# Selections moved behind the squares, and a smaller last step, in a patch-matching convolution kernel

## The chip, the cores and the metric

The kernel runs on one core of one Trainium2 chip. A core has five engines that run side by side, each through its own instructions in order: TensorE (PE in the profile; its weight loads are PEld), VectorE (DVE), ScalarE (ACT), GpSimd (POOL) and SyncE (SP). The last two mostly issue transfers here, which 16 DMA engines carry out. TensorE writes its products to a small memory of eight banks, PSUM, from which ScalarE or VectorE must copy them before a bank is used again.

The metric is the time of one execution in microseconds on the device. The kernel before took 7137.65 us (median of 11 runs, 7121.78 to 7152.27).

## The reference

Eight images of 32 channels and 128 x 128 pixels pass through two layers. What matters here is the first:

```
xb = _patch_match_stack(x)                    # x normalised; 8 shifted copies: 256 channels
dct = _conv(xb, dct_w, groups=C)
h = relu(_conv(_conv(xb, w1), w2, groups=CK, pad=1))
h = relu(_conv(_conv(h, w3), w4, groups=CK, pad=1))
wiener = sigmoid(_conv(_conv(h, w5), w6, groups=CK, pad=1))
filt = _conv(wiener * dct, inv_dct_w, groups=C)
x = x + _conv(filt, agg_w)
```

The patch match looks, for each pixel, at 25 offsets (dy, dx from -2 to 2), sums the squared difference to the shifted image over the channels and over a 3x3 patch, takes the 8 offsets of least cost, and gathers the 8 shifted copies. w1, w3 and w5 are pointwise (1x1, 256 to 256 channels), w2, w4 and w6 are 3x3 filters of one channel each. The second layer normalises the result by groups of channels, filters every channel with one 5x5 kernel and adds that.

## The kernel before

**Tiling.** The rows of an image are worked off eight at a time (R = 8); 16 such steps (NS = 16) and a seventeenth, n = NS, make an image. The seventeenth is there because a 3x3 filter needs the row below: stage i (1, 2, 3: one pointwise and one 3x3 filter each) lags the input by i rows in all, so that the last step has only i rows of stage i left to put out. The steps of all images form one list; step s of the outer loop runs stage 1 on step s, stage 2 on step s - 1, stage 3 on step s - 2, and the end (stage "0") on step s - 2. So around a change of image the stages work on different images, and there is one step of the outer loop in which stage 1 does its n = NS, one for stage 2 and one for stage 3.

**Substeps.** A step of the outer loop has four substeps, i = 3, 2, 1, 0. The order of what TensorE, VectorE and ScalarE do is the order in which the program emits it (`manual_schedule`); GpSimd and SyncE get theirs from a scheduler. A substep i of 3, 2, 1 emits:

- `pointwise_v` (TensorE pv, L637; ScalarE copies tv, L645): the pointwise product for channels 128 to 255, and the first tap of their 3x3 filter (ScalarE, L685);
- waiting small tasks of TensorE (queue "P"), and the cost matmuls pd of the squares made before (queue "Q");
- **the selection** (`gather_select`, ScalarE L584 and L585) for unit u + 1, and the loads of unit u + 3 (`gather_load`, GpSimd L570 for ib, L555 for xt);
- `tick`: a share of the patch match of the next image on VectorE (queue "D"), among it the differences df (L410), in pairs; n = 0 to 2 of an image hold the most of them;
- the other eight taps on VectorE (L688), 128 channels of eight rows each;
- `pointwise_t` (TensorE p, L660; ScalarE copies t, L667; SyncE transfers t<-t, L670 and L672): the pointwise product for channels 0 to 127, laid out by rows in four groups of 32 partitions;
- `gather_pixels` for unit u (TensorE pg, L599; ScalarE copy xb, L606): 88 small products of the shifted pixels with the selection;
- the 3x3 filter of channels 0 to 127 of the substep before, on TensorE (pw, L709), into two banks that exist once (`ps_dw`, one buffer for each of two tags);
- the squares of df (queue "A", ScalarE L418); the relu or sigmoid of the substep before for channels 128 to 255 (ScalarE L692);
- **the evictions** of pw through relu or sigmoid (ScalarE L721), which free those two banks.

Substep 3 has no pw (the substep before it, 0, has no 3x3 part). In substep 0, TensorE multiplies with the dct (pc, L757; the product with acc on VectorE, L760), then does pw of stage 1, and pg behind it; the final products pa (L773) come in the next substep.

**Units.** A gather unit is four rows and four of the eight copies. Units are numbered through; u counts one on in every substep. Step n = NS has none, so that for one step per image nothing is gathered. A selection turns the index tile ib (loaded from DRAM for all 128 partitions; five buffers) into a 0/1 tile sel (four buffers): `ib = (ib - partition)^2`, then `sel = relu(1 - ib)`, for two tiles of 128 x 1024 each. The selection for unit u + 1 is made one substep ahead of its pg.

The emission around the change, before:

```
run("Q")
if s < len(steps):
    unit(gather_select, u + 1)
    unit(gather_load, u + 3)
    tick(b, i)
```

**The last step before.** At n = NS `pointwise_t` works on one row of each of four row groups (nb = 1), of which i - 1 count; the rest of t is set to zero by GpSimd (L669). `depthwise_v` filters four rows, of which i count. `depthwise_t` computes, for u = 0 and 1, two rows each (`[:, :, :nb]`), four in all.

Of the kernel before, what the change touches and what calls it, by code (L numbers as in the profile page):

```python
# [17 lines left out]
C, K, H, W = 32, 8, 128, 128  # L18
CK = C * K
NO = 25  # L20
R = 8
NS = H // R
# [21 lines left out]
def bm3d_conv_preact(  # L44
# [16 lines left out]
    nc = tc.nc  # L61
# [85 lines left out]
    with tc.tile_pool(name="setup", bufs=1) as sp, tc.tile_pool(  # L147
# [3 lines left out]
        for n, w in enumerate((w2, w4, w6)):  # L151
# [6 lines left out]
            for u in range(2):  # L158
                for dy in range(3):
                    s = slice(C * (u + dy), C * (u + dy + 1))  # L160
# [10 lines left out]
        for name, w in (("w1", w1), ("w3", w3), ("w5", w5)):  # L171
            t = sp.tile([P, 2, CK], F32, name=f"nat_{name}", tag=f"nat_{name}")
            nc.sync.dma_start(t, w.rearrange("(m p) i a b -> p m (i a b)", p=P))
            if name == "w1":

                nat, t = t, sp.tile([P, 2, CK], F32, name="w1_kc")
# [6 lines left out]
        for name, dst in (("w1", lw1), ("w3", lw3), ("w5", lw5)):  # L183
            for g in range(2):
                ps = spp.tile([P, CK], F32, name=f"ps_{name}_{g}", tag="ps")
# [461 lines left out]
    def pointwise_t(i, b, n, lhsT, src):  # L647
        t = tb[i - 1]
        nb = 2 if n < NS else 1
        if n == NS and i == 1:  # L650
            nc.gpsimd.memset(t[:, :, 2], 0.0)
        else:
            for q in range(2):
                ps = ps_x.tile([P, 2, 2, W], F32, name=f"p{i}_{b}_{n}_{q}", tag="x")
                for e in range(2):
                    s = slice(C * (2 * q + e), C * (2 * q + e + 1))
                    for g in range(2):
                        rows = src(g)
                        for r in range(4):
                            nc.tensor.matmul(  # L660
                                ps[C * r : C * (r + 1), e, :nb],
                                lhsT[:, g, s],
                                rows[:, r : r + 4 * nb - 3 : 4],
                                start=g == 0,
                                stop=g == 1,
                            )
                nc.scalar.copy(t[:, 2 * q : 2 * q + 2, 2 : 2 + nb], ps[:, :, :nb])  # L667
            for r in range(i - 1) if n == 0 else range(i - 1, 4) if n == NS else ():
                nc.gpsimd.memset(t[C * r : C * (r + 1), :, 2], 0.0)  # L669
        nc.sync.dma_start(t[64:P, :, 0:nb], t[0:64, :, 2 : 2 + nb])  # L670
        if nb == 2:
            nc.sync.dma_start(t[0:64, :, 1], t[64:P, :, 2])  # L672

    def depthwise_v(i, b, n):
        v = tv[i - 1]
        nr = R if n < NS else 4
        out_ = accp.tile([P, R, W], F32, name=f"acc{i}_{b}_{n}_1", tag=f"acc{i}1")
        acc = out_[:, :nr]
        for k, (dy, dx) in enumerate(
            ((1, 1), (0, 0), (0, 1), (0, 2), (1, 0), (1, 2), (2, 0), (2, 1), (2, 2))  # L680
        ):
            tap = dwv[:, i - 1, 3 * dy + dx : 3 * dy + dx + 1]
            rows = v[:, dy : dy + nr, dx : dx + W]
            if k == 0:
                nc.scalar.activation(acc, rows, AF.Copy, scale=tap)  # L685
                yield out_
            else:
                nc.vector.scalar_tensor_tensor(  # L688
                    acc, rows, tap, acc, op0=ALU.mult, op1=ALU.add
                )  # L690
        yield
        nc.scalar.activation(acc, acc, funcs[i - 1])  # L692
        yield
        rows_before_v(i, b, n)

    def depthwise_t(i, b, n):
        t = tb[i - 1].rearrange("p q (h k) w -> p q h k w", k=2)
        nb = 2 if n < NS else 1

        pt = [  # L700
            ps_dw.tile([P, 2, 2, W], F32, name=f"pw{i}_{b}_{n}_{u}", tag=f"dw{u}")
            for u in range(2)
        ]
        for u in range(2):
            hi = 96 if u == 0 else P
            for dx in (0, -1, 1):
                xa, xz = max(0, -dx), min(W, W - dx)
                for j in range(4):
                    nc.tensor.matmul(  # L709
                        pt[u][C * j : C * (j + 1), :, :nb, xa:xz],  # L710
                        dwd[0:hi, i - 1, u, j, dx + 1],
                        t[0:hi, j, :, :nb, xa + dx : xz + dx],
                        start=dx == 0,
                        stop=True,
                        skip_group_check=True,
                    )
        yield 1
        acc = accp.tile([P, R, W], F32, name=f"acc{i}_{b}_{n}_0", tag=f"acc{i}0")
        rows = acc.rearrange("p (k e) w -> p e k w", e=4)
        for u in range(2):  # L720
            nc.scalar.activation(rows[:, u:4:2, :nb], pt[u][:, :, :nb], funcs[i - 1])  # L721
        rows_before_t(i, b, n)
        accs[i, b, n][0] = acc

# [131 lines left out]
    steps = [(b, n) for b in range(NB) for n in range(NS + 1)]  # L856
# [7 lines left out]
    lws, funcs = (lw1, lw3, lw5), (AF.Relu, AF.Relu, AF.Sigmoid)  # L864
    accs, fins = {}, {}

    def unit(stage, u):
        if 0 <= u < len(units) and units[u]:
            if stage is gather_load:
                at = (units[u][0], units[u][1] % 8 // 2)  # L870
                until(lambda: at in ready, 4.0)
            stage(*units[u])
# [28 lines left out]
    with tc.manual_schedule(engines=ORDERED):  # L901
        push(prep(0))
        push(mixes())
        xbd[0] = dram.tile([P, 2, H, W], F32, name="xbd_0", tag="xbd")
        for i in range(3):
            nc.gpsimd.memset(tb[i][0:64, :, 0], 0.0)
        for u in range(7):
            unit(gather_load, u)
            unit(gather_select, u - 2)
            unit(gather_pixels, u - 3)  # L910
        u = 4

        dt = dv = kept = iter(())

        later = lambda: None

        for s in range(len(steps) + 2):
            if s < len(steps):
                b, n = steps[s]
                if s == 2:  # L920
                    push(bands())
                if n == (0 if b else 4) and b + 1 < NB:
                    until(lambda: b in ready, 4.0)
                    push(prep(b + 1))
                if n == NS - 1 and b + 1 < NB:
                    until(lambda: b + 1 in ready, 4.0)
                    xbd[b + 1] = dram.tile([P, 2, H, W], F32, name=f"xbd_{b+1}", tag="xbd")
            for i in (3, 2, 1, 0):
                si = s - (i - 1 if i else 2)
                live = 0 <= si < len(steps)  # L930
                new_v = new_t = iter(())
                if live:
                    bi, ni = steps[si]

                if live and i:
                    src = source(i, bi, ni)
                    pointwise_v(i, bi, ni, lws[i - 1], src)
                    new_v, new_t = depthwise_v(i, bi, ni), depthwise_t(i, bi, ni)
                    accs[i, bi, ni] = [None, next(new_v)]
                later()  # L940
                later = lambda: None
                if live and not i:
                    if ni == 0:
                        x1d[bi] = dram.tile([C, H, W], F32, name=f"x1d_{bi}", tag="x1d")
                        stats[bi] = work.tile([P, NS + 1, 6], F32, name=f"stat_{bi}", tag="stat")
                    xr, xf, j0, j1 = fins.pop(si)
                run("P")
                if live and not i:
                    final_dct(bi, ni, accs[3, bi, ni], xf, j0, j1)

                run("Q")
                if s < len(steps):
                    unit(gather_select, u + 1)
                    unit(gather_load, u + 3)
                    tick(b, i)
                next(new_v, None)
                if live and i:
                    pointwise_t(i, bi, ni, lws[i - 1], src)
                next(kept, None)
                if not i:  # L960
                    next(dt, None)
                if s < len(steps):
                    unit(gather_pixels, u)
                    u += 1
                if i:
                    next(dt, None)
                run("A")
                next(dv, None)
                next(dt, None)
                kept, dv, dt = dv, new_v, new_t  # L970
                if live and not i:
                    later = partial(end, bi, ni, xr, j0, j1)
                if not i and 0 <= s - 1 < len(steps):
                    fins[s - 1] = final_load(*steps[s - 1])
        next(kept, None)
        later()
        until(lambda: NB - 1 in done, 4.0)
# [62 lines left out]
```

## Time and profile before

| what | us |
|---|---|
| median of 11 runs | 7137.65 (7121.78 to 7152.27) |
| the profiled execution | 7160.98 |
| its span | 7159.2 |
| TensorE busy in the span | 6716.4 |
| VectorE busy | 5840.3 |
| ScalarE busy | 5064.3 |
| selections, L584 and L585, 1024 each | 1165.5 and 1084.3 |
| copies t, L667, 128 x 512 | 413.3 (768, mean 580 ns) |
| evictions L721, 128 x 512 | 437.8 (768, mean 597 ns) |

The profiler follows one execution. A row of a group gives the line of the program, the engine, the operation, output and input, the shape and the count, then busy time and the mean of one, then the idle time of the engine ahead of it and what ended it. In a wait row the engine and line named first waited for the one behind the arrow; behind the colon stand the total, the number and the longest. In the order of time each row starts with its start and its length; a bracket at its end gives the idle time of that engine ahead of it. "issue" is idle time for which the profile shows no cause. The clock that is granted to TensorE is given as a share of full speed.

Steps take some 55 us where the next image is being matched and 46 us in the last image; around a change of image they take 39 to 53 us.

### The profile page before, as it was taken

To read this page: it belongs to the slowest core of one execution; us is meant where nothing else is said; L and a number is where in the kernel's file an instruction comes from. 1 tells how busy PE (TensorE), PEld (TensorE's weight loads), DVE (VectorE), ACT (ScalarE), POOL (GpSimd) and SP (SyncE) were. 2 spreads that over 40 slices of the span, in tenths; PEclk is the share of its full clock that TensorE was granted. 3 is DMA by queue.
4 is the path that set the end of the run, shared out by engine and by line. 5 is a ranking of instruction groups with operands and counts; after the bars stand their busy time and mean duration, and the time that the engine had idled before them with its cause. 6 is when DMAs were issued, how large, how long until landed. Compare 5 with 4: busy or idle time off the path is not lost. (4 is left out here: it accounts for less than half of the span.)

```text
span 7159.2 us, 229485 instructions
## 1 busy us (share of the span) xinstructions
PE 6716.4 (94%) x100226; PEld 3165.6 (44%) x100226; DVE 5840.3 (82%) x8606; ACT 5064.3 (71%) x6706; POOL 2744.4 (38%) x4599
## 2 busy tenths in 40 slices
PE   4699899999999999999999999999999999999997
PEld 1344444444444444444444444444444444444443
DVE  6689878888888888888888898888988789767775
ACT  4587668677686777867677776877768677676762
POOL 6244336333353343533335333443336333332222
PEclk8799999999999999999999999999999999999999
DMA  3566656666566575656656666565656656555652
GB/s 80 129 145 147 148 131 148 147 146 149 135 150 148 140 161 130 160 142 147 152 124 162 144 149 138 139 158 148 153 133 150 147 142 150 130 142 141 147 136 65
DMA packets 765484, 1007.70 MB, mean 141 GB/s; under 512 B 215008, under 2 KB 578592, under 8 KB 764480
## 3 DMA queue, kind: packets, MB, share of 16 engines
q0 software_dynamic: 378400, 733.67, 41.8%
q1 hardware_dynamic: 381056, 256.86, 16.9%
q8 instruction: 788, 12.91, 0.8%
q10 hardware_dynamic: 5024, 2.49, 0.2%
q14 instruction: 216, 1.77, 0.1%
HBM read 542.24 MB, written 217.01 MB: 106 GB/s over the span
## 5 line engine op out<-in xcount | busy, mean ns | idle before, releaser
L688 DVE SCALAR_TENSOR_TENSOR acc<-tv,dwv,acc 128x1024 f32<-128x1024 f32 (+1 forms) x3264 | 4083.5, 1252 | 224.5 <-ACT acc L685 110.9
L709 PE MATMUL pw<-t,dwd 128*32 128x508 f32 (+6 forms) x19584 | 2191.5, 594 | 167.1 <-DMA t<-t 115.4
L709 PEld LDWEIGHTS pw<-t,dwd 128*32 128x32 f32 (+1 forms) x19584 | 700.8, 112 | 1418.0 <-issue 1237.9
L570 POOL DMA_DIRECT2D ib<-idxd x1024 | 578.9, 566 | 1894.0 <-ACT sel L585 1774.0
L584 ACT ACTIVATE ib<-ib,nplace 128x1024 bf16<-128x1024 bf16 x1024 | 1165.5, 1138 | 25.2 <-DMA ib<-idxd 25.2
L585 ACT ACTIVATE sel<-ib 128x1024 f32<-128x1024 bf16 x1024 | 1084.3, 1059 | 32.6
L660 PE MATMUL p<-acc,lw 128*32 128x256 f32 x17408 | 992.5, 374 | 10.8 <-issue 10.4
L637 PE MATMUL pv<-acc,lw 128*128 128x512 f32 (+1 forms) x2112 | 977.7, 605 | 8.8 <-DVE acc L760 4.8
L606 ACT COPY xb<-pg 128x512 f32<-128x512 f32 x512 | 304.0, 594 | 724.9 <-PE pg L599 724.0
L645 ACT COPY tv<-pv 128x512 f32<-128x512 f32 (+2 forms) x784 | 445.1, 584 | 493.7 <-PE pv L637 473.2
L660 PEld LDWEIGHTS p<-acc,lw 128*32 128x32 f32 x17408 | 560.8, 110 | 430.4 <-issue 82.1
L721 ACT ACTIVATE acc<-pw 128x512 f32<-128x512 f32 (+1 forms) x816 | 453.4, 584 | 354.1 <-PE pw L709 353.9
L599 PEld LDWEIGHTS pg<-sel,xt 128*32 128x32 f32 x45056 | 591.3, 111 | 233.0 <-issue 133.9
L599 PE MATMUL pg<-sel,xt 128*32 128x48 f32 x45056 | 594.6, 206 | 90.5 <-issue 60.8
L780 DVE TENSOR_TENSOR xr<-xr,pa 128x256 f32<-128x256 f32 (+2 forms) x136 | 55.0, 405 | 732.3 <-PE pa L773 732.3
L637 PEld LDWEIGHTS pv<-acc,lw 128*128 128x128 f32 x2112 | 383.3, 192 | 410.6 <-issue 379.7
L410 DVE TENSOR_TENSOR df<-xn 128x786 f32<-128x786 f32 (+2 forms) x576 | 528.5, 967 | 19.0 <-PE pd L425 18.0
L667 ACT COPY t<-p 128x512 f32<-128x512 f32 x800 | 423.6, 571 | 115.9 <-PE p L660 112.5
L418 ACT ACTIVATE df<-df 128x786 f32<-128x786 f32 (+2 forms) x576 | 460.8, 861 | 47.0 <-DVE df L410 45.8
L685 ACT ACTIVATE acc<-tv,dwv 128x1024 f32<-128x1024 f32 (+1 forms) x408 | 459.7, 1127 | 45.8 <-PE pa L773 31.6
L637 PE MATMUL pv<-xb,lw 128*128 128x512 f32 x1024 | 475.8, 607 | 0.0
L757 PE MATMUL pc<-xf,ldct 128*128 128x512 f32 (+2 forms) x1056 | 470.9, 588 | 0.0
(128 smaller groups left out, 6397.6 us busy)
## 6 DMA issues: line engine op xcount, KB each, us to landing
ib<-idxd POOLq DMA_DIRECT2D x1024, 256.0 KB, 4.3
xbd<-xb POOLq DMA_DIRECT2D x128, 1024.0 KB, 7.9
xf<-xbd POOLq DMA_DIRECT2D x480, 256.0 KB, 9.3
t<-t SPq DMA_DIRECT2D x792, 128.0 KB, 4.9
t<-t SPq DMA_DIRECT2D x384, 256.0 KB, 4.9
tv<-tv SPq DMA_DIRECT2D x384, 130.0 KB, 4.1
xt<-xtd POOLq DMA_DIRECT2D x240, 176.0 KB, 5.2
xl<-xs POOLq DMA_DIRECT2D x256, 64.0 KB, 2.7
```

Source lines behind the costliest of these rows:

```text
L410: nc.vector.tensor_sub(df[:, :, ca:cz], xn[:, r0 : r0 + SR, ca:cz], xn[:, r0 + dy : r0 + dy + SR, ca + dx : cz + dx],)
L418: nc.scalar.activation(df[:, :, ca:cz], df[:, :, ca:cz], AF.Square)
L570: nc.gpsimd.dma_start(ib.rearrange("p k y x -> p (k y x)"), idxd[b][s4 // 8, s4 % 8, 4 * k0 : 4 * k0 + 8] .rearrange("k x -> (k x)") .part ...
L584: nc.scalar.activation(ib, ib, AF.Square, bias=nplace)
L585: nc.scalar.activation(sel, ib, AF.Relu, scale=-1.0, bias=1.0)
L599: nc.tensor.matmul(pg[C * j : C * (j + 1), :, xa:xz], xt[:, t], sels[j // 2][:, j % 2, :, xa:xz], start=True, stop=True,)
L637: nc.tensor.matmul(ps[:, :hr], lhsT[:, g, P:CK], src(g)[:, h : h + hr], start=g == 0, stop=g == 1,)
L660: nc.tensor.matmul(ps[C * r : C * (r + 1), e, :nb], lhsT[:, g, s], rows[:, r : r + 4 * nb - 3 : 4], start=g == 0, stop=g == 1,)
L685: nc.scalar.activation(acc, rows, AF.Copy, scale=tap)
L688: nc.vector.scalar_tensor_tensor(acc, rows, tap, acc, op0=ALU.mult, op1=ALU.add)
L709: nc.tensor.matmul(pt[u][C * j : C * (j + 1), :, :nb, xa:xz], dwd[0:hi, i - 1, u, j, dx + 1], t[0:hi, j, :, :nb, xa + dx : xz + dx], start ...
L757: nc.tensor.matmul(ps[:, : z - a], ldct[:, m], xf[:, m, a:z], start=True, stop=True)
```

## The change

The selection of unit u + 1 is emitted later in its substep: behind pg, the squares (`run("A")`) and the activation L692 (`next(dv, None)`), and in front of the evictions L721 (the last `next(dt, None)`). The loads of unit u + 3 stay where they were. At n = NS, `pointwise_t` computes and copies only the i - 1 row groups that count, `depthwise_v` filters i rows in place of four, and `depthwise_t` computes for u = 0 and 1 as many rows as lie among those i: (1, 0) for stage 1, (1, 1) for stage 2, (2, 1) for stage 3.

```
     def pointwise_t(i, b, n, lhsT, src):
         t = tb[i - 1]
         nb = 2 if n < NS else 1
+        nr = 4 if n < NS else i - 1
...
-                        for r in range(4):
+                        for r in range(nr):
                             nc.tensor.matmul(
                                 ps[C * r : C * (r + 1), e, :nb],
...
-                nc.scalar.copy(t[:, 2 * q : 2 * q + 2, 2 : 2 + nb], ps[:, :, :nb])
+                nc.scalar.copy(
+                    t[: C * nr, 2 * q : 2 * q + 2, 2 : 2 + nb], ps[: C * nr, :, :nb]
+                )
...
     def depthwise_v(i, b, n):
         v = tv[i - 1]
-        nr = R if n < NS else 4
+        nr = R if n < NS else i
...
+        nh = [2 if n < NS else (i + 1 - u) // 2 for u in range(2)]
         for u in range(2):
             hi = 96 if u == 0 else P
             for dx in (0, -1, 1):
                 xa, xz = max(0, -dx), min(W, W - dx)
-                for j in range(4):
+                for j in range(4 if nh[u] else 0):
                     nc.tensor.matmul(
-                        pt[u][C * j : C * (j + 1), :, :nb, xa:xz],
+                        pt[u][C * j : C * (j + 1), : nh[u], :nb, xa:xz],
                         dwd[0:hi, i - 1, u, j, dx + 1],
-                        t[0:hi, j, :, :nb, xa + dx : xz + dx],
+                        t[0:hi, j, : nh[u], :nb, xa + dx : xz + dx],
...
         for u in range(2):
-            nc.scalar.activation(rows[:, u:4:2, :nb], pt[u][:, :, :nb], funcs[i - 1])
+            if nh[u]:
+                nc.scalar.activation(
+                    rows[:, u : u + 2 * nh[u] - 1 : 2, :nb], pt[u][:, : nh[u], :nb], funcs[i - 1]
+                )
...
                 run("Q")
                 if s < len(steps):
-                    unit(gather_select, u + 1)
                     unit(gather_load, u + 3)
                     tick(b, i)
...
                 if s < len(steps):
                     unit(gather_pixels, u)
-                    u += 1
                 if i:
                     next(dt, None)
                 run("A")
                 next(dv, None)
+                if s < len(steps):
+                    unit(gather_select, u + 1)
+                    u += 1
                 next(dt, None)
```

More of the change, by code (lines that the diff above doesn't have):

```diff
@@ L649, in pointwise_t @@
         nb = 2 if n < NS else 1
+        nr = 4 if n < NS else i - 1
         if n == NS and i == 1:
@@ L658, in pointwise_t @@
                         rows = src(g)
-                        for r in range(4):
+                        for r in range(nr):
                             nc.tensor.matmul(
@@ L666, in pointwise_t @@
                             )
-                nc.scalar.copy(t[:, 2 * q : 2 * q + 2, 2 : 2 + nb], ps[:, :, :nb])
+                nc.scalar.copy(
+                    t[: C * nr, 2 * q : 2 * q + 2, 2 : 2 + nb], ps[: C * nr, :, :nb]
+                )
             for r in range(i - 1) if n == 0 else range(i - 1, 4) if n == NS else ():
@@ L675, in depthwise_v @@
         v = tv[i - 1]
-        nr = R if n < NS else 4
+        nr = R if n < NS else i
         out_ = accp.tile([P, R, W], F32, name=f"acc{i}_{b}_{n}_1", tag=f"acc{i}1")
@@ L703, in depthwise_t @@
         ]
+        nh = [2 if n < NS else (i + 1 - u) // 2 for u in range(2)]
         for u in range(2):
@@ L707, in depthwise_t @@
                 xa, xz = max(0, -dx), min(W, W - dx)
-                for j in range(4):
+                for j in range(4 if nh[u] else 0):
                     nc.tensor.matmul(
-                        pt[u][C * j : C * (j + 1), :, :nb, xa:xz],
+                        pt[u][C * j : C * (j + 1), : nh[u], :nb, xa:xz],
                         dwd[0:hi, i - 1, u, j, dx + 1],
-                        t[0:hi, j, :, :nb, xa + dx : xz + dx],
+                        t[0:hi, j, : nh[u], :nb, xa + dx : xz + dx],
                         start=dx == 0,
@@ L720, in depthwise_t @@
         for u in range(2):
-            nc.scalar.activation(rows[:, u:4:2, :nb], pt[u][:, :, :nb], funcs[i - 1])
+            if nh[u]:
+                nc.scalar.activation(
+                    rows[:, u : u + 2 * nh[u] - 1 : 2, :nb], pt[u][:, : nh[u], :nb], funcs[i - 1]
+                )
         rows_before_t(i, b, n)
@@ L952, in bm3d_conv_preact @@
                 if s < len(steps):
-                    unit(gather_select, u + 1)
                     unit(gather_load, u + 3)
@@ L963, in bm3d_conv_preact @@
                     unit(gather_pixels, u)
-                    u += 1
                 if i:
@@ L968, in bm3d_conv_preact @@
                 next(dv, None)
+                if s < len(steps):
+                    unit(gather_select, u + 1)
+                    u += 1
                 next(dt, None)
```

## The prediction

> **What bounds the kernel now.** I read the shares of busy time first, then the stretches of the span, then who waited for whom on TensorE, and last single substeps in order of time.
>
> ```profile
> span 7159.2 us, 229485 instructions
> PE 6716.4 (94%) x100226; PEld 3165.6 (44%) x100226; DVE 5840.3 (82%) x8606; ACT 5064.3 (71%) x6706; POOL 2744.4 (38%) x4599
> ```
>
> TensorE is busy 94% of the span. The next view cuts the span at the image changes (length, then busy time of PE, PEld, DVE, ACT, POOL, then the clock granted to TensorE).
>
> ```profile
> 1900.00:2050.00 150.00, 136.45 (x2328) 71.09 (x2319) 123.49 (x133) 122.41 (x171) 71.66 (x118) 0.97 0.54 138
> 2050.00:2760.00 710.00, 691.87 (x10150) 321.26 (x10142) 602.55 (x939) 507.08 (x666) 270.03 (x454) 1.00 0.63 148
> ```
>
> In the body of an image TensorE is 97% busy (691.87 of 710); around an image change 91% (136.45 of 150), and ScalarE 82%. The work of TensorE sets the end, and what can be won is its idle time: some 18 us in each body and 13.5 at each of seven changes. What it waits for between 300 and 7010 us (total, times, longest):
>
> ```profile
> PE pw L709 <- DMA t<-t: 95.9, 43, 7.5
> PE pg L599 <- issue: 60.8, 41, 4.2
> PE pw L709 <- issue: 27.3, 16, 5.4
> PE pw L709 <- DMA tv<-tv: 10.0, 4, 4.2
> ```
>
> The first row is what the change can reach; "issue" waits on nothing that is shown, and I leave it. One such wait, from substep 1 into substep 0 (start, length):
>
> ```profile
> 3089.67 3.63 PE L660 MATMUL p<-xb,lw 128*32 128x256 f32 x64
> 3093.62 1.06 ACT L585 ACTIVATE sel<-ib 128x1024 f32<-128x1024 bf16 x1
> 3094.58 1.05 ACT L667 COPY t<-p 128x512 f32<-128x512 f32 x2
> 3096.30 0.61 SPq L672 DMA_DIRECT2D t<-t  x1
> 3105.85 5.33 PE L709 MATMUL pw<-t,dwd 96*32 96x512 f32 x48 [2.67 <-DMA t<-t]
> ```
>
> The matmuls p end at 3093.30, but the copies t of ScalarE stand behind the selections and end at 3095.63, 2.3 us later; the transfers follow, and the 3x3 matmuls start 2.67 us late.
>
> A wait costs more than its length. In the windows after a wait of 2.84 us (ending at 5695.16) the clock column reads 0.50:
>
> ```profile
> 5690.00:5695.00 5.00, 2.32 (x6) 0.76 (x4) 4.49 (x7) 3.53 (x4) 1.79 (x3) 1.00 1.13 143
> 5695.00:5700.00 5.00, 4.84 (x24) 1.35 (x28) 2.97 (x17) 0.00 (x0) 1.60 (x3) 0.50 0.23 62
> ```
>
> Those 48 matmuls took 8.60 us, where 5.33 is usual. Over all groups of 48 that follow a wait above 0.3 us between 300 and 7010 us, the excess over 5.3 sums to 49.5 us. **A rule weighed:** the Trainium skill, "TensorE: Matmul & The Clock Gate", Part 1, gives the gate a window of about 3.4 us, so that only longer pauses should cost clock. Here pauses of 1.77 and 2.84 us were followed by groups of 7.25 and 8.60 us. By the page, the clock share of the gain below would shrink to the two waits of 6.8 and 7.5 us; I go by the rows.
>
> **The selection, moved.** One unit is two L584 and two L585, 2 x (1138 + 1059) = 4.39 us of ScalarE by their means (4.3 us from first start to last end), in every substep that gathers. It is neither more nor less, and issues no DMA itself. The order of the two builds shows it, in each substep, behind the copies t, the copy xb, the squares and the activation L692, in front of the two L721. The orders of TensorE and VectorE stay, apart from the smaller last step.
>
> *Earlier now:* copies t, xb, squares and L692, by up to 4.3 us, but never before their input. For t the limit is the end of p: a copy that isn't held up ended 0.65 us behind it (second copy at 3125.49, p ending 3125.43). So t gains 2.33 - 0.65 = 1.7 us in the substep shown, and 3.44 - 0.65 = 2.8 at the image changes. The 43 waits average 2.2. I take back 70% of them; the ends are nothing (if the landing, not the issue, is slow: 9.5 us here) and all.
> - Body: 95.9 less 46.3 in the seven change stretches = 49.6 us of waits, and 13.2 us of slow matmuls behind them; 70% of 62.8 is **-44 us** (0 to -63).
>
> *Later now:* the two L721 (they free the bank of the next pw), tv, L685 and with it VectorE's taps; the selection itself, for pg of the next substep; the load of ib (L570) that waits for it. The selection now also stands behind L692, which waits for VectorE's taps (54.2 us in all before), and L721, tv and L685 queue behind both. POOL already waits 1774 us for L585; xt, xr, xf, x1d, xbd, sq and dsum are queued behind it and come up to 4.3 us later, each with a substep or more in hand. On SP some copies tv<-tv move behind a t<-t; nothing waits for these at once.
> - An ordinary substep: 10.3 to 14.4 us of TensorE, ScalarE 9 to 11. In step 3112 to 3164, moving the rows by hand, the selections end at 3119.6, 3132.9, 3142.4, 3154.5; pg stood at 3125.2, 3134.0, 3147.3, 3162.8. Slack is 1 us at the least. Taps of stage 3 start 3.5 us later, and the L760 products end 7 us before pa needs them: covered. Where VectorE delays the squares or L692 (near 2484 and 3320) I find 0.5 to 1.6 us missing. For eight images **+12 us** (0 to +25).
> - In substep 0 the selection used to fill time in which ScalarE had nothing else:
>
> ```profile
> 3749.06 1.06 ACT L585 ACTIVATE sel<-ib 128x1024 f32<-128x1024 bf16 x1
> 3753.63 0.59 ACT L606 COPY xb<-pg 128x512 f32<-128x512 f32 x1 [3.51 <-PE pg L599]
> ```
>
> Now ScalarE idles 4.3 us longer there and does it in substep 3. At an image change, with two pairs of squares in every substep, that cover is gone. By hand from 1891 to 2081 (steps of 39, 47, 51 and 53 us): gone are the waits of 10.3 us and 5.3 of slow matmuls; pw of the last step saves 3.9 (below). New: pg waits 1.1 and 2.5 for its selection where the stage at hand has only the last rows; pw of stage 1 waits 3.9 and 4.3 for its bank, because L721 now stands behind the selection, with 3.8 of slow clock; and the busiest step lengthens by 2.8, since ScalarE ran there from 3753.63 to 3798.85 with no pause, and a fourth selection enters that chain. 18.4 - 19.5 = -1.1 for each of seven: **-8 us**, ends -140 (none of the new waits) and +100 (the new ones, and no old one gone).
> - The first 300 us: selections come behind the index work; 0 to +17 (four times 4.3), and the wait of 13.57 for t shrinks a little: **+2**.
>
> **The last step.** Per image:
> - pw: 48 matmuls of 256 columns took 2.79 us, twelve sets of four side by side, 0.232 each; of 512, 5.33/12 = 0.444. On that line a set of 128 columns takes 0.128. Stage 1: 6 sets, 0.77 (-2.0); stage 2: 12, 1.54 (-1.25); stage 3: 6 + 6, 2.16 (-0.6). Sum -3.9 us, counted above.
> - p: stage 2 issues 16 of 64 matmuls, stage 3 32. The 64 took 1.96 us, 16 sets of 0.122. If the sets shrink but don't get fewer, nothing is won; by the count, 1.5 + 1.0 us; if a lone matmul goes like the transposes px (four in 0.66, 0.165 each), each stage loses 0.7. I take 0 (-20 to +11 over eight), since that is the same operation's own row.
> - VectorE's taps: 751 ns for 512 elements, 1284 for 1024, so 351, 484 and 617 for 128, 256 and 384. Eight taps save 3.2, 2.1 and 1.1 us. Hidden behind TensorE in the body; in the last 100 us, where relu L692 waits 3.8 to 5.5 us for taps, 6.4 us, plus part of the waits of 2.29 and 3.44 for t: **-8**. ScalarE saves one eviction and some columns: hidden.
>
> **Sum:** -44 + 12 - 8 + 2 - 8 = -46 us on the profiled execution of 7160.98 (span 7159.2): 7115. It lay 0.33% above the median of the eleven runs, 7137.65; scaled by that, **7092 us**.
>
> **Rivals.**
> 1. *ScalarE's chain at the image change decides: slower.* From xb of substep 0 to the eviction before pw of stage 1 it ran 45.2 us without a pause; with the fourth selection 49.5, and 5.3 + 1.1 for pw and pg behind it make a step of 55.9, where 52.8 was. It decides once L721 ends more than 3.7 us (the pc matmuls) behind pw of stage 2. For it: those pauses, and four squares in each of these substeps. Against: in the body ScalarE is 71% busy. +14 at each change (+98) with the other four terms (-38) is +60: 7197.
> 2. *The selections fit into waits for pw.* ScalarE waited 353.9 us in front of L721, on pw; half of the new waits at the changes don't come: -10 each, with the other four terms -108: 7030.
> 3. *One wait for another.* t arrives in time, but landing stays slow or pg waits instead: 7138.
>
> **How the numbers follow.** Two times of this kernel tell 0.2% (14 us) apart. My forecast, 7060 to 7122: 0.40. Rival 2 0.20, rival 3 0.15, rival 1 0.25. So faster 0.60, same 0.15, slower 0.25. The predicted time is the likeliest's; the range takes in most of rivals 1 and 2, 7005 to 7190.
>
> **What will show it.** pw waiting for t<-t falls from 95.9 towards 30 us, and t copies end 0.7 us behind p in substeps 1 and 2. New rows: pg waiting for L585, pw waiting for L721. Steps after an image change lengthen by some 3 us. ScalarE's wait in front of xb grows from 724 us by up to 4.3 in each of 128 steps. pw's last-step groups take 0.8, 1.5 and 2.2 us, p's stay at 1.96. I am wrong if the new waits at the changes exceed 20 us each, or if the t waits stay though the copies come earlier.

## The result, and the profile after

| | median, us | lowest to highest | runs |
|---|---|---|---|
| before | 7134.34 | 7112.30 to 7160.68 | 52 |
| after | 7154.02 | 7143.22 to 7172.23 | 14 |

The ratio of after to before is 1.0032, with a 95% interval of 1.0022 to 1.0042: slower by 0.32%, some 23 us. (The two medians are 20 us apart.) The prediction said faster, by 0.6%.

The profiled execution of after took 7157.50 us. The first two lines of its page are these:

```profile
span 7155.7 us, 227907 instructions
PE 6683.4 (93%) x99394; PEld 3145.3 (44%) x99394; DVE 5788.3 (81%) x8606; ACT 5042.9 (70%) x6698; POOL 2732.8 (38%) x4599
```

TensorE has 33 us less work than in the profile of before, and still the kernel takes longer. (Lines moved a little: pw is L714 now, the evictions L727, the first tap L688, the other taps L691, the relu L695, p L661, the copies t L668, the product with the dct L768, pa L781.) What TensorE waits for between 300 and 7010 us (total, times, longest):

```profile
PE pg L599 <- ACT sel L585: 37.7, 35, 1.8
PE pi L534 <- DVE o L525: 37.4, 18, 3.8
...
PE pw L714 <- ACT acc L727: 33.8, 18, 3.2
PE pw L714 <- DMA t<-t: 30.5, 17, 8.1
PE pg L599 <- ACT tv L645: 30.5, 33, 2.3
PE p L661 <- ACT tv L645: 20.2, 14, 2.2
```

The waits for t fell from 95.9 to 30.5 us, as forecast. In their place stand five rows of which the profile of before has only 1.9 us, for pi: pg for its selection and pw for its bank, which the prediction named, and three that it did not name: pi (the transpose of the index tile o, which VectorE makes when a sort is done) for VectorE, and pg and p for the copies tv, which now hold the shared banks of PSUM longer. On VectorE the first row is of before, the second of after:

```profile
DVE acc L688 <- ACT acc L685: 104.2, 92, 4.8
```

```profile
DVE acc L691 <- ACT acc L688: 317.1, 114, 6.8
```

VectorE waits 213 us longer for the first tap of ScalarE. Most of that is only moved: its wait for pa (L780, L788 in after) fell from 722.3 to 521.0 us. Where it hurts is seen in a table of steps. A step runs from one pa to the next; n counts them in an image, and is three behind the n of the program's loop; each number is the sum of the stretch's steps in us, averaged over the second to the seventh image of one profile. The names of the stretches are rough. In before, 16 to 19 of the next image's squares are made in each of n = 15 and 16 and four to six in n = 0 to 7; its costs are sorted (VectorE L502, L503) in n = 0 to 10, most of them from 8 on; n = 13 to 16 is the change of image.

| kernel | "squares", n 0 to 4 | "sorting", n 5 to 11 | change, n 13 to 16 |
|---|---|---|---|
| before | 280.9 | 346.6 | 189.2 |
| last step alone (e2, below) | 280.9 | 343.4 | 190.1 |
| after | 275.8 | 353.5 | 191.5 |
| early in substep 0 alone (e5, below) | 274.5 | 342.9 | 185.6 |

The move won 5 us for each image in the squares and lost 7 to 10 in the sorting. Here is one sorting step of each kernel, n = 10 of the same image, where the two differ most. First before, the order of time on ScalarE and then on VectorE (start, length; a bracket gives the idle time ahead; the last row of a view counts only the taps up to the view's end, of eight in all):

```profile
5198.69 1.08 ACT L721 ACTIVATE acc<-pw 128x512 f32<-128x512 f32 x2
...
5201.84 1.15 ACT L685 ACTIVATE acc<-tv,dwv 128x1024 f32<-128x1024 f32 x1 [0.49 <-PE pa L773]
5202.90 0.47 ACT L495 COPY ct<-pt 128x400 f32<-128x400 f32 x1
```

```profile
5203.40 0.21 DVE L502 MAX8 mx<-ct 128x8 f32<-128x25 f32 x1 [0.73 <-ACT ct L495]
...
5206.74 5.23 DVE L688 SCALAR_TENSOR_TENSOR acc<-tv,dwv,acc 128x1024 f32<-128x1024 f32 x4
```

The same step of after, from the end of the selection on, again ScalarE and then VectorE:

```profile
5210.95 1.06 ACT L585 ACTIVATE sel<-ib 128x1024 f32<-128x1024 bf16 x1
...
5213.98 1.15 ACT L688 ACTIVATE acc<-tv,dwv 128x1024 f32<-128x1024 f32 x1
5215.03 0.47 ACT L495 COPY ct<-pt 128x400 f32<-128x400 f32 x1
```

```profile
5215.54 0.20 DVE L502 MAX8 mx<-ct 128x8 f32<-128x25 f32 x1 [3.81 <-ACT ct L495]
...
5218.86 3.90 DVE L691 SCALAR_TENSOR_TENSOR acc<-tv,dwv,acc 128x1024 f32<-128x1024 f32 x3
```

Counted from pa (5200.66 before, 5209.70 after), ct starts 2.24 us behind it in before and 5.33 in after, because the selection of substep 0 stands in front of the evictions, tv, the first tap and ct. VectorE has nothing else to do and starts its taps 9.2 in place of 6.1 us after pa. It never makes that up: later in this step TensorE waits for it. VectorE and TensorE in before, where pi finds its input ready and the products with the dct end 1.9 us before the next pa:

```profile
5233.56 0.42 DVE L525 TENSOR_TENSOR o<-o,cst 128x256 f32<-128x256 f32 x1
...
5244.34 2.47 DVE L760 TENSOR_TENSOR acc<-acc,pc 128x512 f32<-128x512 f32 x4
```

```profile
5234.64 0.44 PE L534 MATMUL pi<-cst,o 128*128 128x128 f32 x2
...
5248.71 1.07 PE L773 MATMUL pa<-acc,lagg 128*32 128x256 f32 x16
```

And in after, where pi waits 3.65 us for o, and pc and pw wait behind it on TensorE:

```profile
5230.96 10.51 DVE L691 SCALAR_TENSOR_TENSOR acc<-tv,dwv,acc 128x1024 f32<-128x1024 f32 x8
...
5245.67 0.43 DVE L525 TENSOR_TENSOR o<-o,cst 128x256 f32<-128x256 f32 x1
```

```profile
5246.24 0.43 PE L534 MATMUL pi<-cst,o 128*128 128x128 f32 x2 [3.65 <-DVE o L525]
```

The step took 51.8 us; before it was 48.0. The busy time of VectorE is 42.7 us in both. In before that is 89% of the step, so 5 us are all that may be lost at its start. The eight matmuls pc behind the wait took 5.29 us, where they took 3.60 in before.

### The profile page after: what moved, and what is told of

It reads as the page before. It is cut to its first block, busy times and chain, and to the rows that moved or that the text cites. A ratio compares the mean times of both kernels' runs of the same rounds, so it can differ in the third digit from the quotient of the medians.

```text
span 7155.7 us, 227907 instructions
## 1 busy us (share of the span) xinstructions
PE 6683.4 (93%) x99394; PEld 3145.3 (44%) x99394; DVE 5788.3 (81%) x8606; ACT 5042.9 (70%) x6698; POOL 2732.8 (38%) x4599
## 5 line engine op out<-in xcount | busy, mean ns | idle before, releaser
L691 DVE SCALAR_TENSOR_TENSOR acc<-tv,dwv,acc 128x1024 f32<-128x1024 f32 (+3 forms) x3264 | 4030.8, 1237 | 440.2 <-ACT acc L688 325.7
L714 PE MATMUL pw<-t,dwd 96*32 96x508 f32 (+6 forms) x19392 | 2134.5, 587 | 92.1 <-DMA t<-t 36.8
L714 PEld LDWEIGHTS pw<-t,dwd 96*32 96x32 f32 (+1 forms) x19392 | 679.5, 111 | 1312.0 <-issue 1223.6
L661 PE MATMUL p<-acc,lw 128*32 128x256 f32 x16768 | 988.7, 379 | 26.8 <-ACT tv L645 19.5
L661 PEld LDWEIGHTS p<-acc,lw 128*32 128x32 f32 x16768 | 555.8, 110 | 452.6 <-issue 63.2
L668 ACT COPY t<-p 128x512 f32<-128x512 f32 x800 | 438.9, 577 | 306.4 <-PE p L661 300.5
L695 ACT ACTIVATE acc<-acc 128x1024 f32<-128x1024 f32 (+3 forms) x408 | 415.2, 1018 | 188.3 <-DVE acc L691 188.1
L788 DVE TENSOR_TENSOR xr<-xr,pa 128x256 f32<-128x256 f32 (+2 forms) x136 | 55.0, 404 | 551.9 <-PE pa L781 532.2
L645 ACT COPY tv<-pv 128x512 f32<-128x512 f32 (+2 forms) x784 | 421.6, 582 | 102.8 <-PE pv L637 100.9
L688 ACT ACTIVATE acc<-tv,dwv 128x1024 f32<-128x1024 f32 (+3 forms) x408 | 454.6, 1114 | 22.7 <-PE pa L781 9.1
```

What stands on the lines that cost most here:

```text
L661: nc.tensor.matmul(ps[C * r : C * (r + 1), e, :nb], lhsT[:, g, s], rows[:, r : r + 4 * nb - 3 : 4], start=g == 0, stop=g == 1,)
L691: nc.vector.scalar_tensor_tensor(acc, rows, tap, acc, op0=ALU.mult, op1=ALU.add)
L714: nc.tensor.matmul(pt[u][C * j : C * (j + 1), : nh[u], :nb, xa:xz], dwd[0:hi, i - 1, u, j, dx + 1], t[0:hi, j, : nh[u], :nb, xa + dx : xz ...
```

## The experiments

The change has two parts, and the first can be made in each substep by itself. "Early" is the place of before, "late" that of the change. All ratios are to the kernel before on the same chip, with 95% intervals.

| run | last step | early in | late in | median, us | ratio |
|---|---|---|---|---|---|
| e2_last_only | small | all | none | 7136.23 | 1.0002 (0.9990 to 1.0014) |
| e1_sel_only | as before | none | all | 7178.43 | 1.0065 (1.0048 to 1.0082) |
| after | small | none | all | 7154.02 | 1.0032 (1.0022 to 1.0042) |
| e3_late_21 | small | 3, 0 | 2, 1 | 7078.98 | 0.9924 (0.9905 to 0.9942) |
| e4_late_30 | small | 2, 1 | 3, 0 | 7300.69 | 1.0235 (1.0215 to 1.0254) |
| e5_late_321 | small | 0 | 3, 2, 1 | 7045.35 | 0.9878 (0.9861 to 0.9894) |
| e6_late_210 | small | 3 | 2, 1, 0 | 7437.18 | 1.0425 (1.0404 to 1.0445) |
| f2_late_321_old_last | as before | 0 | 3, 2, 1 | 7053.09 | 0.9874 (0.9853 to 0.9895) |

**The two parts, each alone.** The edits: the hunks of the change on the selection without those on the last step, and the reverse.

> The selection is moved in all four substeps, the last step is as before. Theory A (the move loses; the smaller last step gains the 31 us by which TensorE's busy time fell, and hides part of the loss): the move alone costs 20 + 31 = some 50 us, 7165 to 7200. Theory B (the move is worth about nothing, and the smaller last step brought the loss, by some wait that it opened at the image changes): 7125 to 7145. Theory C (my prediction's sum for the move, -44 + 12 - 8 + 31 of pw counted in it + 2 = about nothing or a gain): 7100 to 7140.

> The smaller last step alone, the selection in its old place. Theory A: TensorE's work falls by 8 x 3.9 = 31 us plus some of p, and the end of the last image by 8: 7090 to 7110. Theory B: slower than before, 7145 to 7165.

The move alone loses 0.65%, some 46 us, as theory A says. But the smaller last step alone is worth nothing, which no theory said. The groups shrank as they should; the time went into a wait. The same place at the change of image, before and then with the small last step (stage 2's pw, and behind pc stage 1's, of which the first view shows 28 matmuls of 48):

```profile
4549.22 2.79 PE L709 MATMUL pw<-t,dwd 96*32 96x256 f32 x48
...
4557.18 3.20 PE L709 MATMUL pw<-t,dwd 96*32 96x512 f32 x28 [1.54 <-DMA t<-t]
```

```profile
4535.45 1.51 PE L714 MATMUL pw<-t,dwd 96*32 96x128 f32 x48
...
4543.71 5.33 PE L714 MATMUL pw<-t,dwd 96*32 96x512 f32 x48 [3.12 <-DMA t<-t]
```

1.3 us less of pw, 1.6 us more of waiting: stage 1's pw starts when t lands, and t stands behind the selection. From the end of p, which is t's input, to that pw it is 8.8 us in before (4548.37 to 4557.18) and 9.0 with the small step (4534.71 to 4543.71). Over the seven changes this wait is 1.6 us on average in before and 3.1 with the small step, and the 48 matmuls behind it took 7 us or more at one change in before and at five with the small step. So for stage 2 the gain was lost twice over: its step, n = 14, got 2.3 us longer. Of the 1.9 us saved in stage 1's group its step, n = 13, shows 1.0; of the 0.6 in stage 3's, n = 15 shows nothing.

**Which substep.**

```
 if s < len(steps):
+    if i in (3, 0):             # e3; e4: (2, 1); e5: (0,); e6: (3,)
+        unit(gather_select, u + 1)
     unit(gather_load, u + 3)
...
 if s < len(steps):
-    unit(gather_select, u + 1)
+    if i not in (3, 0):
+        unit(gather_select, u + 1)
     u += 1
```

> Smaller last step; the selection late in substeps 2 and 1 only, early in 3 and 0. Theory A1 (the loss comes from substep 0, where the selection left time in which ScalarE had nothing else and now stands in front of the copies tv and the first tap of substep 3, so that VectorE's taps start late): the waits of pw for t after substeps 2 and 1 are still saved, the loss is gone: 7050 to 7090, the fastest of the four. Rival A2 (the loss is wherever the selection stands in front of the evictions, in each substep alike): half of the 50 us lost by the move stays: 7115 to 7130.

> Smaller last step; the selection late in substeps 3 and 0 only, early in 2 and 1. Theory A1: it keeps all of the loss and none of the gain, 7140 to 7180, at least as slow as the changed kernel. Rival A2: half of the loss of the move, 7115 to 7130, the same as with substeps 2 and 1.

> As the changed kernel, but in substep 0 the selection is in its old place. Theory 1 (the move loses in substep 0: there the selection used to run in a pause of ScalarE, and late it stands in front of tv, the first tap and the copies ct of substep 3, for which VectorE and TensorE wait): as fast as with substeps 2 and 1 alone, or faster, 7060 to 7095. Theory 2 (it loses in substep 3, where no eviction follows and the selection runs into tv of substep 2): 7135 to 7170, as the changed kernel.

> As the changed kernel, but in substep 3 the selection is in its old place. Theory 1: the loss of substep 0 stays, 7140 to 7170. Theory 2: 7060 to 7095. Theory 3 (two selections that follow one another with little between them lose, as with substep 3 late and 2 early, which measured 7300): here the pair is substep 0 late and 3 early, 7200 or more.

e3 lies where theory A1 put it, e4 far above its 7180. Substep 0 it is: with that one early and the others late the kernel takes 7045 us, 1.2% less than before, and moving it late as well costs 1.0032 - 0.9878 = 1.5%, 110 us. Of the five rows of the result, pi for VectorE is nearly gone (37.4 to 5.0 us); pg for its selection, and pg and p for tv, fall to about a third (37.7 to 12.8, 30.5 to 10.6, 20.2 to 7.7); pw for its bank stays (33.8 to 30.2), so it does not come from substep 0. TensorE and VectorE in e5, the same views as above:

```profile
PE pw L714 <- DMA t<-t: 32.3, 13, 5.7
PE pw L714 <- ACT acc L727: 30.2, 16, 3.2
...
PE pg L599 <- ACT tv L645: 10.6, 7, 1.9
...
PE pi L534 <- DVE o L525: 5.0, 6, 2.6
```

```profile
DVE acc L691 <- ACT acc L688: 145.7, 123, 6.1
```

The placings do not add up: late in 3 and 0, or early in 3 alone, is far worse than all late. There two selections follow one another with little in between, which is theory 3 of e6. The waits of pw for t are 123.8 us in e4 and 135.9 in e6, where before has 95.9 and after 30.5. ScalarE in e6, from substep 0 into 3:

```profile
4358.63 1.14 ACT L584 ACTIVATE ib<-ib,nplace 128x1024 bf16<-128x1024 bf16 x1
...
4366.01 0.47 ACT L495 COPY ct<-pt 128x400 f32<-128x400 f32 x1
4366.39 1.15 ACT L584 ACTIVATE ib<-ib,nplace 128x1024 bf16<-128x1024 bf16 x1
...
4370.66 1.05 ACT L668 COPY t<-p 128x512 f32<-128x512 f32 x2
```

p of this substep ended at 4365.02, and its copies t start at 4370.66: behind two selections. TensorE's next p stands 1.71 us for their banks, and the next pw 1.40 for t.

**The place within a substep, and the worth of the last step.** e7 and e8 put the selection right behind the copies t, in front of xb: e7 in substep 3 (2 and 1 late), e8 in 3, 2 and 1; f1 does so only in an image's first step, the rest as e5. All three are early in substep 0 and have the small last step.

```
 if live and i:
     pointwise_t(i, bi, ni, lws[i - 1], src)
+if s < len(steps) and i in (3,):     # e8: (3, 2, 1); f1: i and n == 0
+    unit(gather_select, u + 1)
```

> Smaller last step; substeps 2 and 1 late, substep 0 early, and in substep 3 the selection right behind the copies t, in front of the copy xb. Theory 1: tv, first tap and ct of substep 3 stay in front of it as in the old place, and t of substep 3 is no longer held up, so some of the 30 us of waits of pw for t that substeps 2 and 1 left go: 7060 to 7080. Rival (those waits come from the transfers or from other work in front of the copies): 7079 +-10, or worse, where xb is late for the bank of the next product.

> Smaller last step; in substeps 3, 2 and 1 the selection right behind the copies t, in substep 0 in its old place. If all of the gain of the move comes from the copies t being earlier, this has it too and gives up none of the rest: 7050 to 7080. If the gain comes also from squares, relu or xb being earlier (no row of before shows that much of it): 7085 to 7125.

> Substep 0 early; substeps 3, 2 and 1 late as in the run of 7045, except in the first step of an image, where they come right behind the copies t as in the run of 7051. In the two traces the step from the fifteenth to the sixteenth pa of an image (while the next image begins) took 45.8 and 41.5 us on average, the ordinary steps with squares 55.7 and 58.1. If each placing keeps its own step: 7045 less 7 x 3.5 to 4.3, 7010 to 7030. If the steps before and after give it back (53.3 against 52.6 one step later): 7035 to 7055.

> The last step as before, the selection early in substep 0 and late in 3, 2 and 1. The smaller last step was worth nothing with all selections early (7136 against 7135) and some 24 us with all late (7154 against 7178). If its worth depends on t no longer being late behind the selection: 7045 + 24 = 7060 to 7085. If it depends on something that substep 0's selection does: 7040 to 7055.

e7 took 7098.98 us (0.9957, 0.9939 to 0.9974), e8 7050.51 (0.9877, 0.9863 to 0.9892), f1 7058.83 (0.9876, 0.9856 to 0.9895). e8 does as well as late, as it should if the gain is t being earlier; but equal times alone don't show that, for its waits differ both ways: 55.0 us of pd waiting for the squares df, where e5 has 1.5, and less of pw for t (20.3 against 32.3) and for its bank (10.1 against 30.2). e7 missed: it has the same waits for df, 52.5 us (e3 has 9.3), without the gain at the banks (30.6). In both the selection of substep 3 stands right in front of the squares. f1 gained nothing; its step at the change took 45.3 us and not 41.5, and why e8 was shorter there the traces don't tell. f2 says that the small last step is worth nothing here too, 7053 without it, 7045 with it, ratios 0.9874 and 0.9878: the second of the two cases that were expected, that its worth hangs on something that substep 0's selection does. Only with all selections late did it bring anything (1.0065 to 1.0032); what that something is, no run shows.

**What in substep 0.** f3 is after with substep 0's selection behind the evictions, the last of the substep; f4 is e5 with one of its two tiles early and the other late.

```
 next(dv, None)
-if s < len(steps):
+if s < len(steps) and i:
     unit(gather_select, u + 1)
     u += 1
 next(dt, None)
+if s < len(steps) and not i:
+    unit(gather_select, u + 1)
+    u += 1
```

```
-    unit(gather_select, u + 1)
+    unit(gather_select, u + 1, (0, 1) if i else (1,))     # f4; tile 0 at the early place
```

> As the changed kernel, but in substep 0 the selection comes behind the evictions of stage 1, the last of the substep. Theory 1 (tv, first tap and ct of substep 3 are late behind it): they stay late, 7140 to 7170. Rival (what counts are the evictions behind the selection, which free the banks for pw): 7045 to 7090.

> As the run of 7045 (3, 2, 1 late), but in substep 0 one of the two tiles of the selection is made early and one late, so that tv, first tap and ct of substep 3 come 2.2 us later and not 4.4. If the loss of 109 us goes with the delay: 7045 + 40 to 65, 7085 to 7110. If slack takes up the first half: 7045 to 7070. If any selection at this place costs all: 7140 or more.

f3 took 7135.53 us (0.9984, 0.9973 to 0.9996), f4 7068.14 (0.9895, 0.9876 to 0.9914). Behind the evictions the selection still costs 0.9984 - 0.9878 = 1.06% of the 1.54%; the third that is left came through the evictions. Half a selection costs 0.17%, within the intervals of the two, and not half of 1.54%: slack takes up most of the first 2.2 us.

**Where in an image, and whether VectorE sets the end.** g1 and g2 are e5 with substep 0 late in one stretch alone (the n of these edits is the loop's; a selection late in one step delays the start of the next, so g1's 7 to 13 reach the table's steps 5 to 11). g3 is after and g4 is e5 with six taps in stage 3.

```
-if i == 0:
+if i == 0 and not 7 <= n <= 13:     # g1; g2: i == 0 and 2 < n < 16
     unit(gather_select, u + 1)
```

```
+if i == 3 and k > 5:                # g3, g4: in the loop over the taps
+    continue
```

> As the run of 7045 (late in 3, 2, 1), with substep 0 late as well, but only in the steps n = 7 to 13 of an image, that is in the stretch where VectorE sorts the costs of the next image. Summed over the steps of the two traces, the changed kernel lost there 10.7 us for each of seven images against the run of 7045, 75 in all. If the loss is VectorE's there: 7105 to 7130. If it is ScalarE's chain around the change of image (my rival 1): 7045 to 7070.

> The same with substep 0 late only in the steps n = 16, 0, 1 and 2, around the change of image, where the traces show 5.9 us for each of seven, 41 in all. If the stretch of sorting carries most: 7075 to 7100. If the change of image carries most (rival 1): 7120 to 7145.

> The changed kernel with six of the nine taps in stage 3 (the last three are left out), 3 x 1.28 = 3.9 us of VectorE less in each step. Theory 1 (in the stretch of sorting VectorE's late start sets the end of the step): most of the 75 us come back, 7080 to 7110. Rival (TensorE waits there for banks of the pool that the late copies tv hold, and VectorE has time): 7135 to 7155.

> The same six taps in the run of 7045 (substep 0 early), to show what the taps are worth where VectorE is not late. Theory 1: little, 7020 to 7045, as VectorE waits there for pa in nearly every step. If it falls by as much as the changed kernel does with six taps, the taps prove nothing about substep 0.

| run | median, us | ratio |
|---|---|---|
| g1_late0_index | 7108.50 | 0.9954 (0.9938 to 0.9970) |
| g2_late0_change | 7107.37 | 0.9954 (0.9938 to 0.9970) |
| g3_six_taps | 7082.91 | 0.9921 (0.9899 to 0.9944) |
| g4_six_taps_early0 | 7034.70 | 0.9849 (0.9824 to 0.9875) |

Each stretch alone costs 0.9954 - 0.9878 = 0.76%, some 54 us, and together they make the 110. I had expected the sorting to carry most; the change of image carries as much. The taps tell what is VectorE's: leaving out three of them is worth 1.11% where substep 0 is late and 0.29% where it is early. The difference, 0.82%, is 58 us (each of the four ratios to some 0.2%), about g1's loss; the rest does not hang on those taps. The profiles agree, one of each: with six taps the sorting falls from 353.5 to 343.6 us for each image and the change stays, 191.5 and 191.2; g1 has 353.2 and 185.3, g2 343.8 and 191.2. The row that goes with the sorting's loss is pi: 37.4 us in after, 36.4 in g1, 29.0 in f3, and 9.6 in g2, 5.0 in e5, 4.5 in g3. The rival that g3 named, the banks held by tv, is not it: with six taps pg and p still wait 25.0 and 20.0 us for tv (30.5 and 20.2 in after).

At the change the traces show ScalarE behind it. ScalarE in after there, then TensorE:

```profile
3746.24 1.06 ACT L585 ACTIVATE sel<-ib 128x1024 f32<-128x1024 bf16 x1
3747.20 1.06 ACT L727 ACTIVATE acc<-pw 128x512 f32<-128x512 f32 x2
```

```profile
3710.48 1.92 PE L599 MATMUL pg<-sel,xt 128*32 128x48 f32 x84 [1.85 <-ACT sel L585]
...
3735.14 1.12 PE L599 MATMUL pg<-sel,xt 128*32 128x48 f32 x88 [1.14 <-ACT tv L645]
...
3747.83 7.03 PE L714 MATMUL pw<-t,dwd 96*32 96x512 f32 x48 [2.96 <-ACT acc L727]
```

Four squares stand in each of these substeps, ScalarE runs without a pause, and TensorE waits in turn for the selection, for a bank held by tv, and for the eviction behind the selection of substep 1. Only part of this is substep 0's: in e5 the first wait is gone from this step (2.8 us for each change in after), while the last stays as it is (2.5 us in both). Moving substep 0's selection behind the evictions does not help here (191.8 us for each change in f3). No run takes the waits at the change apart further.

**The best of them.** The places that did best, together: early in 0, late in 3, right behind the copies t in 2 and 1.

```
+if s < len(steps) and i in (2, 1):     # behind pointwise_t
+    unit(gather_select, u + 1)
```

> Smaller last step; early in substep 0, late in 3, and in 2 and 1 right behind the copies t. The runs with the middle place in substep 3 have 52 and 55 us of waits of pd for the squares df, which the run of 7045 (late in 3) has not; the run with the middle place in 2 and 1 has 10 us of waits of pw for L727 against 30, and 20 against 32 for t. If each placing keeps its own part: 7045 less 20 to 32, 7010 to 7030. If nothing is left to win there: 7040 to 7060.

It took 7026.86 us, a ratio of 0.9849 (0.9829 to 0.9869): faster than before by 1.5% and than after by 1.8%. Its pd waits for df are 10.2 us, and those of pw for L727 8.1: each placing kept its own part, as expected. Against e5 the intervals overlap a little.

## Why the prediction was wrong

**The waits for t: right.** The copy follows its matmuls at once; in after p ends at 3087.07 and the second copy at 3087.73, 0.66 us later, where the prediction had 0.65. The row fell to 30.5 us, and the squares, where most of these waits in the body were, got 5.1 us shorter for each image; -44 us over eight is 5.5.

**"Taps of stage 3 start 3.5 us later, and the L760 products end 7 us before pa needs them: covered": here it failed.** The delay was right, 3.1 us in the step shown, and so was the slack where it was read: in that step of before (n = 3) the products end at 3160.11 and pa starts at 3167.45. But it was taken for all steps, and pa for the only thing on TensorE that needs VectorE in time. That step has no pi. In the sorting, TensorE stops at pi until VectorE has made o, and o comes behind the taps that start late; in the step shown pi had 0.7 us in hand and the products 1.9. The +12 us for ordinary substeps should have been about 54 for substep 0 alone (g1). Of these, pi itself waits 31 to 32 us (37.4 in after and 36.4 in g1, 5.0 in e5); the rest is smaller waits and slow matmuls behind them, which no run takes apart. VectorE's share of busy time would not have warned: 45.44 of 51.80 us, 88%, in the step that was read and 42.72 of 48.05, 89%, in the sorting step. The Trainium skill, "Perfetto Trace Analysis", section Optimization Strategy, says that a kernel may have several regimes, with another engine most in demand in each, and that gaps are to be looked up within the regime. Looking within the sorting would have shown pi; but the mark that the page gives does not tell these two steps apart, since TensorE is the busiest in both (51.80 us of 51.80, and 47.21 of 48.05).

**The image changes, -8: the new waits right in kind, the sign wrong.** The four waits that were foreseen came (pg 1.3 and 2.8 us for each change, where 1.1 and 2.5 were forecast; pw 2.5 and 1.2, forecast 3.9 and 4.3), and the two busiest steps lengthened by 2.4 and 2.6 us, where 2.8 was forecast for one. In the table of steps the change got 2.3 us longer than in before, and 1.4 longer than in e2, where -1.1 was forecast: +10 to +16 for seven in place of -8. One term was too large on its face: the change read by hand had 10.3 us of waits for t, the most of the seven, and was taken for all, 72 us, while the prediction's own sum for the seven is 46.3, or 6.6 each. With that the forecast is +2.6 for each change, +18 for seven. Against substep 0 early the late place costs 54 us around the change (g2), a choice which the prediction did not weigh.

**The last step, -3.9 for each image and -8 at the end: nothing.** The sizes were right (pw takes 0.86, 1.51 and 2.15 us; p 1.9, where 1.96 was forecast), but little of it lay on the path: in e2, behind stage 2's group, stage 1's pw waits for t as much longer, and its matmuls are slow more often. I had counted a smaller group as a gain without asking what the next group on its engine waits for.

**Small terms that I missed on the other side.** In one profile each, the first pa came 12 us sooner than in before (forecast: 2 later), and the last image, in which nothing is matched, took 13.6 less. By the profiles of e2 and after, the squares, the sorting, the change, the start and the last image make (-5.1 + 10.1 + 1.4) x 7 images - 11 - 10 = +24 us; the ratios 1.0002 and 1.0032 make it 21.

**The rivals.** The first, that ScalarE's chain at the change decides, had the right sign with 14 us for each change, six times the 2.3 that after shows against before. The second, that selections fit into the waits for pw, said 7030, and with substeps 3, 2 and 1 late the kernel came to 7045; but pw still waits 30.2 us for its bank there, so the time is near and its reason is not shown. The third happened in part: t did not stay late, but pg did wait instead, 37.7 us for its selection. Its time, 7138, is the nearest of the three to the 7154 measured, though it named neither pi nor tv.

## What to carry to other kernels

An instruction moved later in an engine's queue delays all that is queued behind it, also in the next stage of the loop; the slack of these has to be looked up in every kind of step, for every instruction that waits for them and not for the last one alone. When one move is made at several places of a loop, try each place by itself: here three gained 1.2%, the fourth lost 1.5%, and one put back so that two selections came close together lost another 4%. Work that is taken from the busiest engine is a gain only if what it does next has its input by then.

## What the runs showed of the hardware

Short pauses cost TensorE clock, not always, but with odds that rise with their length. Taking the groups of 48 matmuls pw that take 5.33 us, between 300 and 7010 us, and calling one slow above 6 us, in the profiles of before, after and e5 together: behind less than 0.3 us of pause 7 of 982 were slow, behind 0.3 to 1.5 us 5 of 53, behind 1.5 to 3 us 33 of 60, behind 3 to 4 us 9 of 10, and behind more than 4 us all 9. It isn't fixed by the length alone: the wait of 2.96 us shown of after was followed by 7.03 us (granted clock 0.54 between 3747.8 and 3751.0), that of 3.12 in e2 by 5.33. A third wait for t in before, of 3.80 us (and 7.03 behind it), belongs with the two of 6.8 and 7.5 us that the prediction set apart as long ones.

One kernel's executions scatter more than some of the effects here: before took 7112.30 to 7160.68 us over 52 runs, and the profile that the prediction was worked from, at 7160.98, lay at the top of these. Its span exceeds that of e2, whose median is the same, by 29 us. The waits marked "issue", which the profile ties to nothing, do not explain it: for pg they are 60.8 us in before and 53.1 in e2, but over pg, pw, p and pv together 101.5 and 99.2. What does stays open.
